# Layer 0 of a four-layer convolution network: the last 1x1 convolution on two pixel rows at once, with whole image rows for residual and result

## The chip, the cores and the metric

The kernel runs on one core of a Trainium2 chip. The metric is the device time of one execution in microseconds (us). A core has five engines, each with its own instruction queue that runs in order: TensorE (PE, with its weight loads PEld) multiplies matrices and writes PSUM, VectorE (DVE) and ScalarE (ACT) work element by element, GpSimd (POOL) and SyncE (SP) here mainly issue transfers (DMAs) between HBM and SBUF, the on-chip memory. An engine that waits holds up everything behind it in its own queue.

## The reference

Four layers, each `x = x + conv(groupnorm(x))`, on `x` of shape (4, 64, 256, 256) in f32. Only layer 0 is touched. Cut to what matters:

```python
x = einsum('bchw,oc->bohw', x, w_in)            # 64 -> 384 channels
xp = x in patches of 8 x 8
x = irfft2(rfft2(xp) * fft_filter), patches put back
x = conv(x, w_dw, 3x3, depthwise)
x1, x2 = split(x, 2, axis=1)
x = gelu(x1) * x2                               # 192 channels
return einsum('bchw,oc->bohw', x, w_out)        # 192 -> 64 channels
```

The layer's output is added to its input. Layer 1 then needs the mean and variance of that sum, so the kernel collects statistics of it while it is still on the chip.

## The kernel before

An image of 256 x 256 is 32 rows of 32 patches. Layer 0 works on 12 blocks (three for each image, `blocks`, index `p`), each of 11 rows of patches that begin one patch row apart from the image's edge (`i0` is -1, 10 or 21), so first and last blocks are cut at the edge: some pixel rows of them have 10 patch rows and not 11. Filter and depthwise convolution are one linear map from a patch (and its neighbours) to a patch, done as matrix products with the 64 pixels of a patch on the partitions.

For each block, four times (`kb`, 48 channel pairs each):

- `expand` (lines 444 to 463), for up to 12 patch rows `t`: PE multiplies the normalised input by `w_in` into two PSUM tiles; ACT copies one and DVE the other into `u` (L459 for even `t`, L461 to L463 for odd). Four PSUM tags (`p0` to `p3`, two banks each) go round, so the next `t` but one waits for these copies.
- `convolve` (L494, L503), for 12 groups `g`: 32 matmuls into two PSUM tiles, ACT takes the gelu (L510), DVE multiplies (L511), POOL stores the gated result to `g` in HBM (L514), one row of 374 = 11 x 34 columns for each of 64 pixels and 192 channels. `load_w` (L471) brings the weights three groups ahead.

The last convolution of block p-1 is worked into block p as 16 units (`unit`, `project`), one after `convolve` at g = 1, 4, 7 and 10. A unit is one pixel row `r` of the 8 in a patch and one half of its 8 pixels. `load_half` brings what a unit needs: the residual `r` (L559, one pixel row, the left half of the image's columns on partitions 0 to 63, the right half on 64 to 127) and `g` (L546, L550). A unit runs 16 matmuls (L591 with all 128 partitions, L598 with 64); each reads two pixels of up to 11 patch rows in runs of 8 columns, and writes every second word of PSUM, so that the result lies in the order of the image. DVE adds it to the residual (L607, or L610 and L612), three instructions of statistics follow after every second unit (L618), and POOL stores the row (L622). Each residual row or result is moved in pieces of 128 columns, 512 bytes.

After the last block a tail runs the 16 units of block 11 with nothing beside them (loop `p == NB`), with up to three pixel rows loaded ahead, on SP's and ACT's queues. Layer 1 begins behind it.

The order on PE, DVE, ACT and SP is the order of the program (`manual_schedule`), so where a call stands decides what stands ahead of it in each queue.

Of the kernel before, what the change touches and what calls it, by code (L numbers as in the profile page):

```python
# [17 lines left out]
C = 64  # L18
HID = 192
# [74 lines left out]
def _layouts(i):  # L94
# [6 lines left out]
    by_class = np.concatenate([turn[:, 0:2].ravel(), turn[:, 2].ravel()])  # L101
# [20 lines left out]
class _Net:  # L122
# [152 lines left out]
    def _layer0(self, ctx, dst):  # L275
# [36 lines left out]
        wts = [dr.tile([2, 64, 2, Q, NC], F32, name=f"wt{t}") for t in range(HID // C)]  # L312
# [63 lines left out]
        def weights(t, copies):  # L376

            for hh in range(2):
# [13 lines left out]
                for h in range(2):  # L392
                    for k, cols in ((0, [(0, 0, C), (C, 96, NC - C)]), (1, [(0, Q, NC)])):
                        for n0, c0, n in cols:
                            nc.gpsimd.dma_start(
                                wts[t][h, 32 * hh : 32 * hh + 32, k, :, n0 : n0 + n].rearrange("i c n -> c i n"),
                                T[quarters[2 * h + k], :, :, c0 : c0 + n].rearrange("p a b n -> p (a b) n"),
                            )
# [4 lines left out]
        xns, x0, wl, st, gs, bst0s, bst1, loads, rts = ({} for _ in range(9))  # L403
        xr = lambda v: v.rearrange("c (i r) w -> r c i w", r=P)
# [60 lines left out]
        def load_w(j):  # L465

            p, k = divmod(j, HID // 8)
            if p >= NB:
                return
            w = wl[j] = p_w.tile([128, 2, 4, NC], F32, tag="w", name=f"w_{j}")  # L470
            nc.sync.dma_start(  # L471
                w, wts[k // 8][:, :, :, 4 * (k % 8) : 4 * (k % 8) + 4].rearrange("h i k c n -> (h i) k c n")
            )
# [11 lines left out]
        def convolve(p, kb, g):  # L485
# [5 lines left out]
            for k in range(2):  # L491
                for c in range(2):
                    for h in range(2):
                        nc.tensor.matmul(  # L494
                            out(C * c, C, k, h), w[halves[h], k, 2 * (G % 2) + c, 0:C], cells(h, 4 * g + 2 * k + c, 0, 0),
                            start=True, stop=False, tile_position=(h * C, c * C), skip_group_check=True,
                        )
            for n, (c0, m, down, right) in enumerate(UNITS):
                for k in range(2):
                    for c in range(2):  # L500
                        q = C * c + Q * (1 - k)
                        for h in range(2):
                            nc.tensor.matmul(  # L503
                                out(q, m, k, h), w[halves[h], k, 2 * (G % 2) + c, c0 : c0 + m],
# [14 lines left out]
        def planes(r):  # L519

            if r < 5:
                return [(0, 6 * r, 0, 6), (1, 4 + 2 * r, 6, 2)]
            if r == 5:
                return [(0, 30, 0, 2), (1, 28, 2, 4), (1, 14, 6, 2)]
            return [(1, 16 + 6 * (r - 6), 0, 6), (1, 2 * (r - 6), 6, 2)]

        def rows_in(p, r):
# [3 lines left out]
            return lo, hi, i0 + lo + (r == P - 1), (r + 1) % P  # L531

        def load_g(p, r, half):

            pools, queues = sources[p == NB - 1], (nc.sync, (nc.sync, nc.scalar)[p == NB - 1])
            g1 = pools[0].tile([128, 4, L], F32, tag="g1", name=f"g1_{p}_{r}_{half}")
            g6 = pools[1].tile([128, 2, L], F32, tag="g6", name=f"g6_{p}_{r}_{half}")
            loads[p, r, half] = g1, g6
            q0 = 4 * half
            for x, p0, q, n in planes(r):  # L540
                part = lambda lo, m: (max(q, lo), min(q + n, lo + m))
                for k in range(2):
                    at = (x ^ k) * Q + p0 - q
                    lo, hi = part(q0, 4)
                    if lo < hi:
                        queues[k].dma_start(g1[halves[k], lo - q0 : hi - q0], gs[p][k, 0:C, at + lo : at + hi])  # L546
                    for s in range(2):
                        lo, hi = part(q0 + 2 * s, 2)
                        if lo < hi:
                            queues[k].dma_start(  # L550
                                g6[quarters[2 * s + k], lo - q0 - 2 * s : hi - q0 - 2 * s],
                                gs[p][k, C : HID // 2, at + lo : at + hi],
                            )

        def load_r(p, r):
            lo, hi, j0, rr = rows_in(p, r)
            rt = rts[p, r] = sources[p == NB - 1][2].tile([128, NR, HW2], F32, tag="r", name=f"r_{p}_{r}")[:, 0 : hi - lo]
            for s in range(2):
                nc.sync.dma_start(  # L559
                    rt[halves[s]], xr(a["x"][blocks[p][0]])[rr][:, j0 : j0 + hi - lo, s * HW2 : (s + 1) * HW2]  # L560
                )

        def load_half(p, r, half):
            if 0 <= p < NB and r < P:
                if half == 0:
                    load_r(p, r)
                load_g(p, r, half)

        def project(p, r, half):

            b, i0 = blocks[p]
            lo, hi, j0, rr = rows_in(p, r)
            m = hi - lo
            po, rt = banks(f"po_{p}_{r}_{half}"), rts[p, r]
            n = m * 16

            def moving(g, bank, s, x):
                at = lambda q: (O1 + 8 * s, E1 + 1 + 8 * s)[x] if q < 7 else (E1 + 8 * s, O1 + 8 * s)[x]
                o, d = at(2 * bank), at(2 * bank + 1) - at(2 * bank)
                return bass.AP(  # L580
                    tensor=g.tensor, offset=g.offset + lo * CW + o, ap=[g.ap[0], [L + d, 2], [CW, m], [1, 8]]
                )

            out = lambda bank, s, x: po[halves[s], bank, 0 : 2 * n].rearrange(
                "p (q i j x) -> p x q i j", q=2, i=m, x=2
            )[:, x]
            g1, g6 = loads.pop((p, r, half))
            for k in range(2):
                for x in range(2):
                    for s in range(2):  # L590
                        nc.tensor.matmul(  # L591
                            out(k, s, x), wo1, moving(g1[:, 2 * k], 2 * half + k, s, x),
                            start=(x == 0), stop=False, skip_group_check=True,
                        )
            for x in range(2):
                for k in range(2):
                    for s in range(2):
                        nc.tensor.matmul(  # L598
                            out(k, s, x), wo6[halves[k]],
                            moving(g6[halves[k], 0], 2 * half + k, s, x),  # L600
                            start=False, stop=True, tile_position=(k * C, s * C), skip_group_check=True,
                        )
            rv = rt.rearrange("p i (j w) -> p w (i j)", w=P)
            pv = po[:, 0:2, 0 : 2 * n].rearrange("p b (k n) -> p b k n", k=2)
            if half == 0:
                v = rv[:, 1:5].rearrange("p (b k) n -> p b k n", k=2)
                nc.vector.tensor_add(v, v, pv)  # L607
                return
            v = rv[:, 5:7]
            nc.vector.tensor_add(v, v, pv[:, 0])  # L610
            v = bass.AP(tensor=rv.tensor, offset=rv.offset + 7, ap=[rv.ap[0], [-7, 2], rv.ap[2]])
            nc.vector.tensor_add(v, v, pv[:, 1])  # L612
# [3 lines left out]
            for k in range(0, m, 4):  # L616
                v = rt[:, k : min(k + 4, m)].rearrange("p i w -> p (i w)")
# [868 lines left out]
```

## Time and profile before

| | us |
|---|---|
| median of 3 runs | 6655.79 |
| lowest, highest | 6634.38, 6662.45 |
| the profiled execution | 6626.21 |
| its span, first to last instruction | 6624.4 |
| layer 0: first `convolve` starts, last one ends | 146.6, 3937.0 |
| the tail: until the last matmul of L598 ends | 4061.3 |
| first matmul of layer 1 | 4077.8 |

A page of the profile lists busy times by engine, the span in 40 slices, the DMA queues, the chain of work that ended last, and groups of instructions. A matmul in f32 appears as two records. Matmuls on different parts of the array run side by side, so what a group of them costs is read from start to start in the timeline, not from the length of a record. "Idle before" names what an engine waited for. "issue" is idle time for which the profile shows no cause.

| engine in layer 0, 500 to 3500 us | busy us of 3000 |
|---|---|
| PE | 2783 |
| DVE | 1725 |
| ACT | 1251 |
| DMA engines, mean share | 0.78 |

### The profile page before, as it was taken

Reading aid. Unit: us, or ns where it says so; the run is one execution under the profiler, and the core shown is the slowest. Engines: PE = TensorE matmul, PEld = TensorE weight load, DVE = VectorE, ACT = ScalarE, POOL = GpSimd, SP = SyncE. Lnnn points to the kernel's source line nnn. Section 1 sums busy time; section 2 is a strip of 40 time slices with the busy share of each in tenths; the row PEclk is TensorE's granted clock in tenths of the full one; section 3 lists DMA queues with packets and bytes.
Section 4 is the critical chain, followed back from the end, with each engine's and each line's share of the span. In section 5 each row is a group of like instructions: output and inputs, shape, how many; then the busy total and the mean of one; then the engine's idle time right before and its main releaser. Section 6 shows DMA issues by size and latency. Waiting matters only on the chain.

```text
span 6624.4 us, 238282 instructions
## 1 busy us (share of the span) xinstructions
PE 6040.5 (91%) x106712; PEld 3213.7 (49%) x106712; DVE 4275.7 (65%) x5924; ACT 3238.8 (49%) x4564; POOL 1050.4 (16%) x1646
## 2 busy tenths in 40 slices
PE   2999999999999999999999986999899999999987
PEld 1455555555555555555555543333344444443576
DVE  5556555555555555555555545999798898885355
ACT  4454434344434444344444422777777887783211
POOL 3111111111111111111111111111022222221011
PEclk9999999999999999999999997999999999999855
DMA  8577777777878877877767669999666666677889
GB/s 236 152 206 211 216 213 222 218 216 213 230 213 238 219 222 207 223 214 220 210 193 206 188 194 247 232 229 228 165 177 176 168 180 173 173 187 264 318 351 394
DMA packets 878510, 1447.67 MB, mean 219 GB/s; under 512 B 77252, under 2 KB 586452, under 8 KB 875444
## 3 DMA queue, kind: packets, MB, share of 16 engines
q1 hardware_dynamic: 725284, 923.09, 54.8%
q0 software_dynamic: 148672, 500.14, 21.7%
q8 instruction: 843, 13.81, 0.9%
q10 hardware_dynamic: 3536, 9.20, 0.5%
q14 instruction: 175, 1.43, 0.1%
HBM read 932.08 MB, written 500.04 MB: 216 GB/s over the span
## 4 chain that ended last, share of the span: by engine, by line
PE 82%; DMA 6%; ACT 5%; DVE 3%; issue 3%; SPq 0%; POOL 0%; ACTq 0%; DVEq 0%; POOLq 0%
PE pc L503 18%; PE pc L494 12%; PE m L869 10%; PE psu L444 9%; PE one L1110 8%; PE div L1069 6%; PE po L591 4%; ACT u L459 4%; PE psu L450 4%; PE psz L1099 2%; PE po L598 2%; DMA x<-x 2%; PE psa L1297 2%; DMA g<-g 2%; PE psy L1444 1%
## 5 line engine op out<-in xcount | busy, mean ns | idle before, releaser
L511 DVE TENSOR_TENSOR h<-h,pc 128x374 f32<-128x374 f32 x1152 | 574.7, 541 | 1268.7 <-ACT h L510 1267.7
L510 ACT ACTIVATE h<-pc 128x374 f32<-128x374 f32 x1152 | 492.6, 480 | 1824.9 <-PE pc L503 1822.0
L503 PE MATMUL pc<-u,w 64*16 64x374 f32 (+2 forms) x27648 | 1244.1, 483 | 0.0
L494 PE MATMUL pc<-u,w 64*64 64x374 f32 x9216 | 928.6, 494 | 81.1 <-DVE u L463 32.2
L514 POOL DMA_DIRECT2D g<-h x576 | 416.7, 723 | 3111.0 <-DVE h L511 2904.7
L503 PEld LDWEIGHTS pc<-u,w 64*16 64x16 f32 (+2 forms) x27648 | 413.8, 92 | 769.5 <-issue 768.9
L444 PE MATMUL psu<-win,xn 64*128 64x96 f32 x8704 | 627.0, 283 | 131.8 <-ACT u L459 110.5
L459 DVE COPY u<-psu 64x384 f32<-64x384 f32 x1088 | 604.3, 555 | 167.7 <-PE psu L444 155.7
L459 ACT COPY u<-psu 64x384 f32<-64x384 f32 x1088 | 560.0, 515 | 238.9 <-PE psu L444 218.8
L444 PEld LDWEIGHTS psu<-win,xn 64*128 64x128 f32 x8704 | 574.0, 192 | 202.6 <-ACT u L459 143.6
L1055 DVE TENSOR_TENSOR q<-xn 128x2313 f32<-128x2313 f32 (+2 forms) x256 | 627.4, 2492 | 1.7 <-ACT xn L256 1.7
L1110 PE MATMUL one<-z,wp 32*32 32x512 f32 x16384 | 592.1, 596 | 17.8 <-issue 13.6
L494 PEld LDWEIGHTS pc<-u,w 64*64 64x64 f32 x9216 | 350.3, 133 | 531.0 <-issue 354.7
L256 ACT ACTIVATE xn<-x,nb,r 128x1024 f32<-128x1024 f32 (+3 forms) x272 | 486.8, 1793 | 244.6 <-DMA x<-x 140.8
L1056 ACT ACTIVATE q<-q 128x2313 f32<-128x2313 f32 (+2 forms) x256 | 529.0, 2086 | 32.7 <-DVE q L1055 31.2
L450 PE MATMUL psu<-win,xn 64*64 64x96 f32 x17408 | 458.2, 252 | 81.9 <-issue 57.2
L1069 PE MATMUL div<-q,ones 64*32 64x512 f32 x8192 | 466.3, 594 | 12.9 <-ACT q L1056 9.3
L1110 PEld LDWEIGHTS one<-z,wp 32*32 32x32 f32 x16384 | 367.6, 103 | 223.6 <-issue 80.1
L450 PEld LDWEIGHTS psu<-win,xn 64*64 64x64 f32 x17408 | 395.5, 137 | 126.0 <-issue 77.0
L1143 POOL DMA_DIRECT2D x<-r x512 | 275.5, 547 | 969.8 <-DVE r L1140 945.1
L591 PE MATMUL po<-g,wo 128*64 128x176 f32 (+1 forms) x3072 | 315.8, 348 | 63.3 <-DMA g<-g 41.3
L869 PE MATMUL m<-t,wk 64*64 64x512 f32 x3072 | 341.1, 588 | 0.0
(162 smaller groups left out, 6668.1 us busy)
## 6 DMA issues: line engine op xcount, KB each, us to landing
g<-h POOLq DMA_DIRECT2D x576, 374.0 KB, 7.0
x<-x SPq DMA_DIRECT2D x240, 640.0 KB, 6.4
w<-wt SPq DMA_DIRECT2D x288, 448.0 KB, 8.4
x<-x SPq DMA_DIRECT2D x100, 1024.0 KB, 14.2
g<-g SPq DMA_DIRECT2D x414, 187.0 KB, 5.7
g<-g SPq DMA_DIRECT2D x736, 93.5 KB, 6.0
x<-in_x_dram SPq DMA_DIRECT2D x256, 256.0 KB, 8.1
x<-o POOLq DMA_DIRECT2D x128, 512.0 KB, 8.2
```

Source lines behind the costliest of these rows:

```text
L444: nc.tensor.matmul(ps[s][:, k, at], xn[halves[s], n : n + 2].rearrange("p n r w -> p (n r w)"), win[halves[s], kb, 0 : 2 * PB], start=True ...
L450: nc.tensor.matmul(ps[s][halves[1 - odd], k, at], xn[halves[s], n + odd].rearrange("p r w -> p (r w)"), win[halves[s], kb, PB * (1 - odd) ...
L459: copy(at(h, 8 * s + o), v[k, c : c + PB])
L494: nc.tensor.matmul(out(C * c, C, k, h), w[halves[h], k, 2 * (G % 2) + c, 0:C], cells(h, 4 * g + 2 * k + c, 0, 0), start=True, stop=False, ...
L503: nc.tensor.matmul(out(q, m, k, h), w[halves[h], k, 2 * (G % 2) + c, c0 : c0 + m], cells(h, 4 * g + 2 * k + c, down, right), start=False, ...
L511: nc.vector.tensor_mul(h[:, k], h[:, k], ps[k][:, 1, 0:L])
L591: nc.tensor.matmul(out(k, s, x), wo1, moving(g1[:, 2 * k], 2 * half + k, s, x), start=(x == 0), stop=False, skip_group_check=True,)
L869: nc.tensor.matmul(rows2(m)[halves[j], s], w[dx][halves[s]], ts[n][halves[s], i, 2 * j : 2 * j + 2, dx : dx + W], start=(dx == 0), stop=(d ...
L1055: nc.vector.tensor_sub(d, p0, p1)
L1056: nc.scalar.activation(d, d, AF.Square)
L1069: ins = nc.tensor.matmul(ps[quarters[j], h], ones[halves[h]], q[n, g, k][halves[h], r + 2 * j : r + 2 * j + 2, o : o + W], start=(m == 0), ...
L1110: ins = nc.tensor.matmul(rows2(ps[g])[quarters[j], k], w[quarters[i]], z[quarters[i], h, 2 * j + dy : 2 * j + dy + 2, dx : dx + W], tile_p ...
```

## The change

- A unit is now two pixel rows (`r` = 2k and 2k+1) and two of the 8 pixels. Row 2k goes to the lower 64 partitions of PSUM, row 2k+1 to the upper. `project` runs 8 matmuls, each over a whole gated row of 374 columns, and writes 374 columns in one piece; pad columns are computed too and left in PSUM. DVE picks the wanted columns out when it adds: two instructions for each unit, four where the two rows have different patch rows (the last pair of rows in first and last blocks).
- Residual and result tiles hold whole image rows (1024 bytes), one tile for four units, with one buffer in place of two of half the size (in the tail two in place of three). `load_r` stands in `expand` at t = 8, not at a unit.
- `load_g` brings four transfers for most units; one takes 96 partitions and one 32. The order of rows in `w_out` (`by_class`) follows.
- The statistics of a tile (six, or twelve where the rows differ) are put in a list (`tasks`) and taken from it: two after each `convolve` that has no unit behind it, one after each `t` of `expand`. Units now follow g = 0, 3, 6 and 9; the tile is complete at g = 9, so the list is taken at g = 10 (two), g = 11 (two), t = 0 and t = 1 (one each).
- The weights lie in HBM so that a load reads 3584 bytes in one piece and not two of 1792.

```diff
-        wts = [dr.tile([2, 64, 2, Q, NC], F32, name=f"wt{t}") for t in range(HID // C)]
+        wts = [dr.tile([2, 64, Q, 2, NC], F32, name=f"wt{t}") for t in range(HID // C)]
...
+        def load_g(p, n):
+            if not (0 <= p < NB and n < 16):
+                return
+            rr, q0 = (2 * (n // 4), 2 * (n // 4) + 1), 2 * (n % 4)
+            last = p == NB - 1
+            pools, queues = sources[last], (nc.sync, (nc.sync, nc.scalar)[last])
+            g1 = pools[0].tile([128, 2, 2 * L], F32, tag="g1", name=f"g1_{p}_{n}")
+            g6 = pools[1].tile([128, 2, L], F32, tag="g6", name=f"g6_{p}_{n}")
+            loads[p, n] = g1, g6
+            parts = [(g1[Q:128], 1, slice(0, HID // 2), q0, 2), (g1[0:Q], 0, slice(C, HID // 2), q0, 2)]
+            parts += [(g6[halves[q]], 0, slice(0, C), q0 + q, 1) for q in range(2)]
...
+        def load_r(p, n):
+            if not (0 <= p < NB and n < P // 2):
+                return
+            rt = rts[p, n] = sources[p == NB - 1][2].tile([128, NR, W], F32, tag="r", name=f"r_{p}_{n}")
             for s in range(2):
+                lo, hi, j0, rr = rows_in(p, 2 * n + s)
+                nc.sync.dma_start(rt[halves[s], lo:hi], xr(a["x"][blocks[p][0]])[rr][:, j0 + lo : j0 + hi])
...
+            for q in range(2):
+                for s in range(2):
+                    nc.tensor.matmul(
+                        po[halves[s], q, 0:L], wo1, g1[:, s, q * L : (q + 1) * L],
+                        start=True, stop=False, skip_group_check=True,
+                    )
+            for q in range(2):
+                for s in range(2):
+                    nc.tensor.matmul(
+                        po[halves[s], q, 0:L], wo6[halves[q]], g6[halves[q], s],
+                        start=False, stop=True, tile_position=(q * C, s * C), skip_group_check=True,
+                    )
...
+                    v = bass.AP(
+                        tensor=v.tensor, offset=v.offset + lo * CW + even,
+                        ap=[v.ap[0], [CW, m], [odd - even, 2], [1, W // P // 2]],
+                    )
+                    o = rt[h, lo:hi].rearrange("p i (j x w) -> p w i x j", x=2, w=P)[:, (q0 + q + 1) % P]
+                    nc.vector.tensor_add(o, o, v)
+            if n % 4 < 3:
                 return
+            for side in sides:
+                h, lo, hi, j0, rr = side
+                nc.gpsimd.dma_start(xr(dst[b])[rr][:, j0 + lo : j0 + hi], rt[h, lo:hi])
...
+            tasks.extend((stats, next(slot), c) for c in chunks)
...
-            p_r = pool("l0r", 2, side="right")
+            p_r = pool("l0r", 1, side="right")
...
-                    sources.append([pool("l0g1e", 6), pool("l0g6e", 6), pool("l0re", 3)])
-                    ahead = 3
+                    sources.append([pool("l0g1e", 6), pool("l0g6e", 6), pool("l0re", 2)])
+                    ahead = 6
+                    for n in range(2):
+                        load_r(p - 1, n)
...
                         if 0 <= i0 + t < NP:
                             expand(p, kb, t)
+                        task()
+                        if t == 8:
+                            load_r(p - 1, kb)
...
-                        if g in (1, 4, 7, 10):
+                        if g in (0, 3, 6, 9):
                             unit()
+                        else:
+                            task(2)
```

## The prediction

> **What bounds the kernel now.** I read the slices and the chain first. PE is busy through layer 0 (slices 2 to 24), and the chain of what ended last is mostly PE.
>
> ```profile
> PE   2999999999999999999999986999899999999987
> ...
> PE pc L503 18%; PE pc L494 12%; PE m L869 10%; PE psu L444 9%; PE one L1110 8%; PE div L1069 6%; PE po L591 4%; ACT u L459 4%; PE psu L450 4%; PE psz L1099 2%; PE po L598 2%; DMA x<-x 2%; PE psa L1297 2%; DMA g<-g 2%; PE psy L1444 1%
> ```
>
> Then the table of stretches, to separate the loop (first row) from the tail (second). Columns after the window: its length, then busy us of PE, PEld, DVE, ACT, POOL; granted clock, DMA share, GB/s.
>
> ```profile
> 500.00:3500.00 3000.00, 2783.34 (x53660) 1579.50 (x53662) 1724.83 (x3021) 1250.62 (x2468) 449.56 (x606) 0.98 0.78 216
> 3949.00:4062.00 113.00, 61.24 (x512) 37.90 (x512) 34.45 (x44) 0.00 (x0) 11.32 (x17) 0.59 1.02 248
> ```
>
> In the loop PE is the bound, in the tail DMA (1.02). Where PE idles in the loop is in PE's waits from 430 to 3900 us: inside `expand`, and at the first matmul behind it, always on the copies or on "issue". No DMA is among its larger waits.
>
> ```profile
> PE psu L444 <- ACT u L459: 99.2, 152, 1.5
> PE psu L450 <- issue: 54.6, 46, 4.2
> PE pc L494 <- DVE u L459: 28.3, 15, 2.0
> PE pc L494 <- DVE u L463: 27.1, 27, 1.3
> ```
>
> So PE sets the pace in `convolve` and in units; in `expand` it is the ring PE, copies, PE. A second of work saved on PE in a unit counts in full. A second added to DVE counts in `expand` and hardly elsewhere.
>
> **The matmuls of a unit.** PE's timeline, start to start. A unit of 11 patch rows, one of 10, and in layer 1 matmuls with 512 columns in long runs:
>
> ```profile
> 1181.91 1.62 PE L591 MATMUL po<-g,wo 128*64 128x176 f32 x16
> 1183.46 0.93 PE L598 MATMUL po<-g,wo 64*64 64x176 f32 x16
> 1184.21 1.48 PE L494 MATMUL pc<-u,w 64*64 64x374 f32 x16
> ```
>
> ```profile
> 432.04 1.48 PE L591 MATMUL po<-g,wo 128*64 128x160 f32 x16
> 433.45 0.86 PE L598 MATMUL po<-g,wo 64*64 64x160 f32 x16
> 434.13 1.48 PE L494 MATMUL pc<-u,w 64*64 64x374 f32 x16
> ```
>
> ```profile
> 4255.18 1.04 PE L869 MATMUL m<-t,wg 64*64 64x512 f32 x8
> 4256.04 1.04 PE L869 MATMUL m<-t,wi 64*64 64x512 f32 x8
> ```
>
> A unit costs 1184.21 - 1181.91 = 2.30 us, or 434.13 - 432.04 = 2.09. L591's 16 records go two side by side (8 rounds of 1.55/8 = 0.194 us for 176 columns; one by one they would take 0.55 ns a column, less than any row here), L598's four side by side (4 rounds). The new unit has 8 and 8 records: 4 + 2 = 6 rounds of 374 columns. In layer 1, 8 records are 2 rounds of 0.43 us, 0.84 ns a column, so 374 cost 0.314 and the unit 6 x 0.314 = 1.89. The other end: a `convolve` takes 3.52 us (1187.69 to 1191.22) for 10 rounds of 374 columns in runs of 17, 0.352 a round, unit 2.11. I take 1.89, since the new rows are read and written in one run, as in layer 1. The loop holds the units of blocks 0 to 10: 176, of which 62 read 10 rows (31 pixel rows of the four first and three last blocks) and 114 read 11. Saving 114 x 0.41 + 62 x 0.20 = **59 us**; at 2.11 it is 114 x 0.19 - 62 x 0.02 = 20.
>
> **The statistics on DVE.** Before, L618 stands between the product of g = 10 and that of g = 11, where DVE waits for ACT anyway. Now part of it is queued behind the product of g = 11, ahead of the first copies of `expand`. DVE's timeline there, before:
>
> ```profile
> 635.10 1.61 DVE L618 BATCH_NORM_STATS2 bst<-r 128x6 f32<-128x512 f32 x3
> 637.51 1.00 DVE L511 TENSOR_TENSOR h<-h,pc 128x374 f32<-128x374 f32 x2 [0.81 <-ACT h L510]
> 638.98 2.26 DVE L459 COPY u<-psu 64x384 f32<-64x384 f32 x4 [0.47 <-PE psu L444]
> ...
> 643.42 2.26 DVE L459 COPY u<-psu 64x384 f32<-64x384 f32 x4 [0.45 <-PE psu L444]
> ```
>
> A pair of patch rows takes 4.44 us (638.98 to 643.42, and the next at 647.86). The ring is: copies of even t (2.26), PE's next even t (1.96), 0.2 of delay; DVE is idle for 0.45 of each pair. PE starts the next even t only when the copies are done, and the first matmul of `convolve` waits for the last copy, so what delays DVE beyond its idle time is not won back. Two statistics cost 1.28 (L320: 2 in 1.28), one of 256 elements 1.61 - 1.28 = 0.33. With 11 rows: 1.28 - 0.47 = 0.81 ahead of the first copy, then 0.64 + 0.33 - 0.45 = 0.52 behind t = 0 and 1: 1.33. With 10 rows 0.81 + 0.66 - 0.45 = 1.02. Where the last tile has twelve: 2.56 - 0.47 + 0.97 + 0.66 - 0.45 = 3.27. Of the 44 tiles of the loop 43 have an `expand` behind them: 12 x 1.02 + 24 x 1.33 + 7 x 3.27 = 67 us. PE's "issue" stalls (54.6 and 18.7 us, 1.7 for each of these `expand`) let DVE catch up when they fall into the first third: 43/3 x 0.5 = 7. I take **+60**. The ends: 0 if it all goes into other idle time of DVE (1275 of 3000 us in the loop, though most lies in `convolve`); 12 x 1.94 + 24 x 2.25 + 7 x 4.19 = 107 if nothing of it is absorbed.
>
> The adds: 8 x 0.81 (L610, 352 elements) for four units against 2 x (1.46 + 0.81 + 0.81), 6.5 against 6.2, and up to 3 us at once where there are four. They lie beside `convolve` plus unit (3.52 + 1.89 = 5.41) with the product (1.0) and L320 (1.28): 3.9 in 5.4, hidden. Without that cover they would cost what they last, 0.3 x 44 = 13 more than before.
>
> **Loads in the loop.** At zero. SP: `load_r` waits at the head of SP's queue for the tile's stores and statistics, since there is one buffer. The stores go to POOL behind the adds of g = 9, some 4 us after that `convolve`, and land 7.5 us after issue (L622's median; twice the size now, say 10): 8 us into `expand`. The statistics end at about the same time. The load lands 10 us later, at 18 of 28 us, and the first add comes 3.5 + 1.9 us after `expand`: some 15 us in hand. Behind it in SP's queue stand L471 and L546's successors; weights are three groups (21 us) ahead. At a new block the first `load_g` waits for the last store of `g` (before: SP held from 713 to 727 us) and the residual comes behind it; two units and one tile are 3.7 MB, at 248 GB/s 15 us, so 742; the first `convolve` there started at 745.2, the first add comes at 751: 9 us in hand. If the cover is gone, DVE waits, then the products behind it, then ACT's and PE's tiles. The weights' runs, POOL's fewer stores and fewer SP instructions shorten what PE does not wait for.
>
> **The tail.** DMA shares from 3948 to 4062 us (first two rows; packets, MB, share of 16 engines), and of layer 1 from 4200 to 4600 us (third):
>
> ```profile
> q1 hardware_dynamic: 13584, 14.14, 57.1%
> q10 hardware_dynamic: 3456, 8.81, 29.9%
> ```
>
> ```profile
> q1 hardware_dynamic: 50087, 50.03, 65.5%
> ```
>
> q10 carries `g` alone: 0.299 x 16 x 114 us / 3456 = 158 ns for packets of 2549 bytes. Priced by bytes like that, the 9.2 MB of `g` on q1 take 567 of its 1041 us; the 9728 residual packets of 512 bytes have the rest, 49 ns each. In layer 1 a packet of 1000 bytes takes 84 ns. So a 1024-byte row costs 84 to 98 and not 98: 5632 rows x 14 ns / 16 engines = 5 us less. `g` is cut finer (2992 and 1496 bytes; by the line through 49 and 158 ns, 182 and 102): 1.5 us of engine time for each of 16 units, over 16 engines 1.5 more. Two tiles of residual (2.8 MB) are asked for while the last `g` store lands (3937 to 3949 us) in place of 1.45 MB: 1.35 MB / 248 GB/s = 5.5 less. The last twelve statistics (7 us) and adds (3) lie in the 12 us that layer 1 waited for `x` after the last unit. Sum **-9**, between 0 and -20.
>
> [...]
>
> **Sum.** 6626.2 - 59 + 60 - 9 = 6618 for the profiled execution. It stands 29.6 under the median of the runs shown, so 6648 there: **no change that can be told** (0.5%, 33 us, is about what a measurement of this kernel can tell).
>
> **Rivals.** (a) The statistics hide: DVE has 4 to 5 idle us in each `expand`, and PE's stalls give more. For: idle on paper. Against: it comes in pieces of 0.45 that the ring needs. Then 6655.8 - 59 - 9 = 6588. (b) Slower: nothing of them is absorbed, the ring at the start of `expand` takes 107: 6655.8 - 59 + 107 - 9 = 6695. It decides from (33 + 59 + 9) / 43 = 2.35 us for a tile, where I have 1.4. For: every copy that ends `expand` is DVE's (L463, L459). (c) Fewer bytes in flight end PE's "issue" stalls: in block 0, with DMA shares of 0.09 to 0.36 in `expand`, there are none; later, at 0.55 to 0.89, 1.7 us each. Half of 73 gone: 6648 - 37 = 6611. Against: the DMA time of a block falls by some 9 us of 310 (residual 5, weights 24 x 128 packets fewer at 22 ns / 16 = 4). (d) The rows gain less than layer 1's long runs say (unit 2.11, saving 20): 6648 + 39 = 6687.
>
> **Chances and range.** Forecast 0.48; (a) and (c) and their mixes 0.27; (b), (d) and their mix 0.25. Range 6595 to 6700: from near (a) to just above (b). The likeliest one alone: 6625 to 6675.
>
> **What would show it.** Unit start to start 1.89 us (L591's and L598's successors); L618 ahead of L459 at the start of `expand`, and `expand` 1 to 3 us longer from first matmul to the second part of the first L494; tail some 9 us shorter. Wrong if adds wait for the residual, if `expand` is no longer, or if "issue" shrinks.

## The result and the profile after

The changed kernel takes 6811.47 us (median, 6805.40 to 6818.67) against 6658.82 before (6634.38 to 6662.45): 1.024 times, 95% interval 1.0222 to 1.0258, some 153 us slower. The forecast was 6648. The profiled execution spans 6816.8 us against 6624.4, 192.4 more. That is some 40 more than the medians differ: the profiled execution of the kernel before (6626.21) lies under all four of the runs above.

After: the busy slices of PE, and the chain of what ended last, by line (L495 and L504 are the matmuls of `convolve`, L445 and L451 those of `expand`, L582 and L588 those of a unit).

```profile
PE   3999999889999999999999894999999999999987
...
PE pc L504 17%; PE pc L495 12%; PE m L885 10%; PE one L1126 8%; PE psu L445 7%; PE div L1085 6%; PE psu L451 4%; PE po L582 4%; DVE u L460 3%; DMA x<-x 2%; PE psz L1115 2%; PE po L588 2%; DVE bst L618 2%; PE psa L1313 2%; ACT u L460 2%
```

Two entries are new among those shown: copies (L460) and statistics (L618) of DVE. The table of stretches, the loop and then the tail (length; busy us of PE, PEld, DVE, ACT, POOL; granted clock, DMA share, GB/s):

```profile
500.00:3500.00 3000.00, 2717.93 (x48830) 1462.43 (x48832) 1693.36 (x3039) 1193.32 (x2353) 375.41 (x508) 0.95 0.77 207
4113.00:4226.00 113.00, 51.51 (x264) 15.48 (x256) 28.92 (x46) 0.85 (x2) 5.88 (x10) 0.68 1.05 258
```

In the loop PE is busy for 65 us less of 3000 (2783 before), and the granted clock fell from 0.98 to 0.95: PE waits more, and while it works it works more slowly. Where it waits, from 430 to 4100 us (us in total, times, longest):

```profile
PE psu L451 <- issue: 112.8, 50, 4.9
PE psu L445 <- ACT u L460: 64.7, 100, 0.8
PE psu L445 <- DVE u L460: 39.1, 57, 2.2
PE pc L495 <- DVE u L460: 32.1, 16, 2.0
PE psu L445 <- issue: 31.7, 15, 4.0
```

"issue" was 54.6 and 18.7 us before, and the wait of L445 for DVE's copies is as good as new (0.5 us before). Both are in `expand`. From the timelines of both kernels, stretch by stretch: the 44 `expand` of the blocks with units last 1547 us in place of 1346 (+201; first matmul to the second part of the first `convolve`); the stretches between them 2120 in place of 2146 (-26); from the last `convolve` to the first matmul of layer 1 it is 149.4 in place of 140.7 (+9); the start of the loop and layer 1 differ by 2 and 8. So all of the loss is in `expand`, whose code the change hardly touches. Some 30 of the 201 us may come from which executions were profiled: in e7 below, whose `expand` is that of before, it lasts 1378 us in an execution of 6666.74 us.

**One of these `expand`, at 1748 us.** PE's timeline (start, us, instruction; idle before and its releaser), then SP's queue, then a table of stretches with granted clock and DMA share in the third and second column from the end.

```profile
1752.52 0.46 PE L445 MATMUL psu<-win,xn 64*128 64x96 f32 x2 [0.79 <-ACT u L460]
1755.19 2.29 PE L445 MATMUL psu<-win,xn 64*128 64x96 f32 x30 [2.22 <-DVE u L460]
1757.41 3.18 PE L451 MATMUL psu<-win,xn 64*64 64x96 f32 x64
...
1764.36 1.06 PE L451 MATMUL psu<-win,xn 64*64 64x96 f32 x41 [0.47 <-issue]
1765.35 2.33 PE L445 MATMUL psu<-win,xn 64*128 64x96 f32 x32
1767.61 1.37 PE L451 MATMUL psu<-win,xn 64*64 64x96 f32 x53
1773.85 0.90 PE L451 MATMUL psu<-win,xn 64*64 64x96 f32 x11 [4.87 <-issue]
1774.68 3.73 PE L445 MATMUL psu<-win,xn 64*128 64x96 f32 x32
1778.34 2.63 PE L451 MATMUL psu<-win,xn 64*64 64x96 f32 x64
1780.90 2.03 PE L445 MATMUL psu<-win,xn 64*128 64x96 f32 x32
```

```profile
1756.47 4.58 SPq L553 DMA_DIRECT2D g<-g  x8
1761.59 1.73 SPq L565 DMA_DIRECT2D r<-in_x_dram  x2
1764.30 1.46 SPq L472 DMA_DIRECT2D w<-wt  x1
```

```profile
1757.00:1760.00 3.00, 2.93 (x56) 2.50 (x58) 2.88 (x7) 2.07 (x4) 0.00 (x0) 0.50 0.85 205
...
1769.00:1772.00 3.00, 0.00 (x0) 0.00 (x0) 0.97 (x2) 0.71 (x2) 0.00 (x0) 1.00 1.15 202
1772.00:1775.00 3.00, 1.15 (x14) 0.93 (x14) 0.21 (x1) 0.45 (x1) 0.00 (x0) 0.80 1.16 199
1775.00:1778.00 3.00, 3.00 (x32) 3.00 (x30) 1.46 (x3) 1.09 (x3) 0.00 (x0) 0.50 0.54 133
```

Three things are seen. The late copies leave PE idle for 2.22 us at 1753, and the next 64 matmuls take 3.18 us where 1.55 is normal: the clock is 0.50. `g`, residual (1.4 MB) and weights are then asked for within 10 us, the 16 DMA engines are full (1.15), and PE stands for 4.87 us although no semaphore or engine that the trace shows holds it ("issue"). And again the clock is at 0.50 behind it: 32 matmuls in 3.73 us in place of 2.03. Both gaps cost more than their own length: 1.63 us over the 1.55 and 1.70 over the 2.03. In the 44 `expand` the granted clock stood at 0.50 for 352 us, before for 106 (in e7 for 175).

**What "issue" stands for here.** Before, PE's timeline around 1050 us, and the page's line for the queue that carries instructions (packets, MB, share):

```profile
1046.39 0.48 PE L450 MATMUL psu<-win,xn 64*64 64x96 f32 x9
1048.53 1.38 PE L450 MATMUL psu<-win,xn 64*64 64x96 f32 x55 [1.66 <-issue]
1049.84 2.03 PE L444 MATMUL psu<-win,xn 64*128 64x96 f32 x32
1051.80 1.05 PE L450 MATMUL psu<-win,xn 64*64 64x96 f32 x39
1053.87 0.79 PE L450 MATMUL psu<-win,xn 64*64 64x96 f32 x25 [1.02 <-issue]
```

```profile
q8 instruction: 843, 13.81, 0.9%
```

Between the two stalls lie 55 + 32 + 39 = 126 matmuls, as after the change between 1764.36 and the stall of 4.87 us (41 + 32 + 53). The kernel's 106712 matmuls over 843 packets are 127 a packet, and after the change 103640 over 818 are 127 too. So PE stalls where one packet (13.81 MB / 843, 16 KB) of its instructions ends and the next has not come. In `expand` 126 matmuls last 4.3 us (1048.53 to 1052.85), in `convolve`, 64 in 3.52 us, about 6.9.

The profile's records of DMA packets show when such a packet starts. Windows 1045.9 to 1046.0 and 1051.3 to 1051.4 before, then 1764.4 to 1770.75 and 1770.75 to 1770.85 after (packets that start there, MB, share of 16 engines; the third window has no row of q8):

```profile
q8 instruction: 1, 0.02, 63.1%
q8 instruction: 1, 0.02, 66.6%
q1 hardware_dynamic: 1065, 1.35, 110.3%
q8 instruction: 1, 0.02, 86.6%
```

The share, times 16 engines, times the 0.1 us of the window, is how long the packet took: 1.01, 1.07 and 1.39 us. They ended near 1047.0, 1052.4 and 1772.2, and PE went on 1.4 to 1.7 us behind each (1048.53, 1053.87, 1773.85). All 376 stalls of 1.8 us or more put down to "issue" in the 44 `expand` of the 20 traces ended like that, 1.2 to 2.0 us behind the end of such a packet; of all matmuls of `expand` about one in nine stands there. The packet itself is not slow; it starts late. In the third window, 6.4 us from PE's first matmul of one packet, the next has not started, and the engines are full (1.10). Behind all stalls of 0.5 us or more, the next packet starts 1.3 us (median) after PE began the one before it where the DMA engines are under 0.6 busy meanwhile (392 cases), and 4.2 us where they are over 1.1 (155). With the packet's 1.0 to 1.3 us and some 1.45 from its end to the first matmul that makes about 3.8 or 7 us, against the 4.3 us for which a packet lasts in `expand` and the 6.9 in `convolve`.

### The profile page after: what moved, and what is told of

Its sections match the earlier page's. It is cut to its first block, busy times and chain, and to the rows that moved or that the text cites. A ratio compares the mean times of both kernels' runs of the same rounds, so it can differ in the third digit from the quotient of the medians.

```text
span 6816.8 us, 230910 instructions
## 1 busy us (share of the span) xinstructions
PE 6125.5 (90%) x103640; PEld 3143.8 (46%) x103640; DVE 4340.0 (64%) x6132; ACT 3236.8 (47%) x4564; POOL 976.1 (14%) x1550
## 3 DMA queue, kind: packets, MB, share of 16 engines
q1 hardware_dynamic: 641396, 926.12, 54.6%
## 4 chain that ended last, share of the span: by engine, by line
PE 79%; DVE 9%; DMA 6%; issue 4%; ACT 2%; SPq 0%; DVEq 0%; POOLq 0%; ACTq 0%
PE pc L504 17%; PE pc L495 12%; PE m L885 10%; PE one L1126 8%; PE psu L445 7%; PE div L1085 6%; PE psu L451 4%; PE po L582 4%; DVE u L460 3%; DMA x<-x 2%; PE psz L1115 2%; PE po L588 2%; DVE bst L618 2%; PE psa L1313 2%; ACT u L460 2%
## 5 line engine op out<-in xcount | busy, mean ns | idle before, releaser
L504 PE MATMUL pc<-u,w 64*16 64x374 f32 (+2 forms) x27648 | 1239.3, 482 | 0.2 <-issue 0.2
L495 PE MATMUL pc<-u,w 64*64 64x374 f32 x9216 | 928.6, 494 | 80.0 <-DVE u L460 32.1
L445 PE MATMUL psu<-win,xn 64*128 64x96 f32 x8704 | 678.7, 298 | 154.8 <-ACT u L460 75.4
L504 PEld LDWEIGHTS pc<-u,w 64*16 64x16 f32 (+2 forms) x27648 | 412.5, 92 | 766.8 <-issue 766.8
L445 PEld LDWEIGHTS psu<-win,xn 64*128 64x128 f32 x8704 | 617.8, 207 | 230.6 <-ACT u L460 102.3
L460 DVE COPY u<-psu 64x384 f32<-64x384 f32 x1088 | 604.0, 555 | 185.1 <-PE psu L445 171.6
L460 ACT COPY u<-psu 64x384 f32<-64x384 f32 x1088 | 559.6, 514 | 340.5 <-PE psu L445 320.6
L451 PE MATMUL psu<-win,xn 64*64 64x96 f32 x17408 | 521.1, 270 | 153.1 <-issue 113.5
L495 PEld LDWEIGHTS pc<-u,w 64*64 64x64 f32 x9216 | 351.6, 133 | 577.4 <-issue 328.6
L451 PEld LDWEIGHTS psu<-win,xn 64*64 64x64 f32 x17408 | 450.4, 150 | 204.8 <-issue 154.4
L606 DVE TENSOR_TENSOR r<-r,po 128x352 f32<-128x352 f32 (+3 forms) x448 | 317.9, 743 | 213.4 <-PE po L588 144.6
L582 PE MATMUL po<-g,wo 128*64 128x374 f32 x1536 | 294.0, 503 | 57.0 <-DMA g<-g 47.0
## 6 DMA issues: line engine op xcount, KB each, us to landing
x<-in_x_dram SPq DMA_DIRECT2D x256, 256.0 KB, 10.1
```

Source lines behind the costliest of these rows:

```text
L445: nc.tensor.matmul(ps[s][:, k, at], xn[halves[s], n : n + 2].rearrange("p n r w -> p (n r w)"), win[halves[s], kb, 0 : 2 * PB], start=True ...
L451: nc.tensor.matmul(ps[s][halves[1 - odd], k, at], xn[halves[s], n + odd].rearrange("p r w -> p (r w)"), win[halves[s], kb, PB * (1 - odd) ...
L460: copy(at(h, 8 * s + o), v[k, c : c + PB])
L495: nc.tensor.matmul(out(C * c, C, k, h), w[halves[h], 2 * (G % 2) + c, k, 0:C], cells(h, 4 * g + 2 * k + c, 0, 0), start=True, stop=False, ...
L504: nc.tensor.matmul(out(q, m, k, h), w[halves[h], 2 * (G % 2) + c, k, c0 : c0 + m], cells(h, 4 * g + 2 * k + c, down, right), start=False, ...
L582: nc.tensor.matmul(po[halves[s], q, 0:L], wo1, g1[:, s, q * L : (q + 1) * L], start=True, stop=False, skip_group_check=True,)
```

## The experiments

Four theories were tried against each other: the late statistics (L618 ahead of the copies of `expand`); the place of the residual load, in `expand`; its form (whole rows, 704 KB at once, bytes in flight); other parts of the change.

**e1: statistics early, the rest as changed.** `task()` in `expand` is taken out, and

```diff
-                        else:
-                            task(2)
+                        if g == 9:
+                            task(3)
+                        if g == 10:
+                            task(len(tasks))
```

> The changed kernel with the statistics of a residual tile taken where before's were: three behind the product of g=9 and the rest behind that of g=10 (L618), none at g=11 and none between the copies of expand. First theory (the statistics hold up the copies of u, the matmuls of expand wait, and what follows them, the matmuls' lower granted clock and the 'issue' stalls, comes from that): most of the lost time comes back, 6640 to 6690 us against 6811. Second theory (the residual load of 1.4 MB, which the single buffer pushes into a few us of expand, starves the matmuls): little comes back, only the 20 to 50 us in which copies were seen waited for, 6760 to 6795 us, and the 'issue' stalls between 18 and 27 us after the start of an expand stay at over 100 us in all.

6786 us, 1.0224 (1.0198 to 1.0251), an interval that overlaps the changed kernel's. As the second theory has it, but the edit was weak: with the unit still at g=9, DVE now holds back the product of g=11, and PE waits 25 us for `h` at the start of `expand` in place of 39 for the copies. It doesn't clear the statistics.

**e2: no residual loads in the loop.** The first tile is loaded once and all later results are added into it, so the sums are not the reference's. In `load_r`:

```diff
+            if (p, n) > (0, 0) and p < NB - 1:
+                rts[p, n] = rts[0, 0]
+                return
...
```

> The changed kernel without the residual loads of the loop: the first tile is loaded once and all later results of blocks 0 to 10 are added into it and stored from it (only the last block, after the loop, loads its own residuals). Left out are 43 loads of 1.4 MB, so its result is not the reference's. Second theory (the load that falls into expand starves the matmuls): most of the lost time comes back, 6640 to 6700 us, and the 'issue' stalls of expand fall from 148 us to 80 or less. First theory (statistics on VectorE): 6780 to 6810 us, expand stays some 4 us longer than before's.

6663 us, 1.0043 (1.0029 to 1.0056): 131 us of the loss are gone. PE's waits show which:

```profile
PE psu L445 <- DVE u L460: 38.7, 57, 2.2
...
PE psu L451 <- issue: 29.6, 25, 3.3
```

"issue" at L451 falls from 112.8 to 29.6 us; the waits for late copies (38.7) stay, and `expand` is still 55 us longer than before (1401).

**e3: the kernel before with late statistics.** They are put in a list as in the change and taken from it behind g=11 (two) and behind the `t` of `expand` (one each):

```diff
+                        task()
...
+                        if g == 11:
+                            task(2)
+                        elif g < 10:
+                            task(3)
```

> The kernel before with one edit: the three statistics that it takes with the last unit of a kb (at g=10) are put off, two of them behind the product of g=11 and one behind the first copy of the next expand; units, loads and stores stay. First theory: a delay of VectorE at the start of expand is enough by itself to slow what follows, so the time rises by 80 us or more (6740 to 6850). Second theory: it costs only what the copies are late, 3 x 1.1 us in 44 expands less what is absorbed, 20 to 60 us (6680 to 6720).

6662 us, 1.0040 (1.0024 to 1.0056): 27 us, too little for the first theory alone.

**e4: e1 and e2 at once.**

> The changed kernel with both edits: statistics at g=9 and g=10, and the residual loads of the loop left out as in the run without them (its result is not the reference's). Both theories: nothing of the 192 us is left, and the shorter units (2.08 us in place of 2.30 and 2.09) and the shorter tail show, about 40 us under before: 6600 to 6640. If it stays above 6700, a third cause is at work (the units at g=0, the finer loads of g, the result's store as 1.4 MB at once, or the weight runs). If the two single edits give back parts that add up to this one's, the causes are separate; if each alone gives back nearly all, they are one chain.

6662 us, 1.0045 (1.0030 to 1.0061), the same as e2 and not 40 under before: something else costs, too. PE's waits for `h` (25 us) don't explain it, since e5 below has as many (29) and is 37 us faster. PE's "issue" in the waits is larger, 51.3 + 12.1 us against e5's 29.2 + 4.0; what makes it so isn't shown (the profiled execution is e4's slowest).

**e5: the load in the convolution, all statistics early.** The load waits for the first matmul of g=0, the units move:

```diff
+                        ins = convolve(p, kb, g)
+                        if g == 0:
+                            load_r(p - 1, kb, ins)
...
-                        if g in (0, 3, 6, 9):
+                        if g in (2, 4, 6, 8):
                             unit()
-                        else:
-                            task(2)
+                        if g > 8:
+                            task(3)
```

> The changed kernel with all its residual loads, but each waits for the first matmul of the convolution g=0 instead of being free to start in expand; the units stand behind g=2, 4, 6, 8 and all statistics behind g=9 and g=10. If the place of the 1.4 MB load (in expand) is the cause: 6600 to 6670 us, expand within 60 us of before's 1346 in all, 'issue' stalls of expand at 80 or less. If the load costs wherever it lies (its bytes, or one transfer of 704 KB in place of two of 352): 6740 or more.

6638 us, 0.9989 (0.9975 to 1.0003): with the same bytes and rows the whole loss is gone. `expand` is at 1351, "issue" at L451 is 29.2. The edit moves the load, the units and the statistics at once; e8 and e14 take them apart.

**e6: the kernel before with both residual rows asked for in `expand`**, `load_r(p - 1, r)` for rows 2kb and 2kb + 1 at t=8, none behind the units.

> The kernel before with one edit: the residual loads of both pixel rows of a kb (the same 1.4 MB in the same 352 KB pieces) are put at t=8 of the expand ahead, where the changed kernel has them, instead of behind the units. If the place of the load is the cause: it takes most of the change's loss over, 80 to 160 us on before's 6632 (6710 to 6790), with 'issue' stalls of expand at 120 or more. If the loss needs the changed kernel's larger rows or its later statistics: 6625 to 6660.

6634 us, 0.9985 (0.9971 to 1.0000). A miss: the place alone does not do it. But the load was not as bunched: the first of its four pieces started 4.0 us into `expand` (median of 44), the last at 8.3; the changed kernel's two start at 9.8 and 10.6.

**e7: the kernel before with the weights' layout of the change.**

> The kernel before with the weight layout of the change alone (runs of 3584 bytes). The prediction had it at zero: 6620 to 6645 us. If the 29 us that are left without residual loads come from the weights: 6650 to 6670.

6633 us, 0.9992 (0.9970 to 1.0014): nothing, as predicted.

**e8: e5 with units at g = 3, 5, 7, 9 and the statistics as changed**, `task(2)` at the other g and `task()` in `expand`.

> As the run with the load in the convolution, but units behind g=3, 5, 7, 9, and the statistics taken as the change does (two behind each of the convolutions without a unit, the last of them between the copies of the next expand). The prediction's price of late statistics was 60 us; the kernel before with late statistics lost 27. If they cost that here too: 20 to 60 us over the run with early statistics. If the statistics only cost where the load lies in expand as well: within 10 us of it.

6697 us, 1.0080 (1.0056 to 1.0103): 59 us over e5. This is the price of late statistics without the load, units one group later included, and PE's wait for DVE is back (2.5 us in e5):

```profile
PE psu L445 <- DVE u L460: 37.2, 58, 3.1
```

**e9: the kernel before, both rows gated on the first matmul of t=3** (`self.after(d, ins)`).

> The kernel before with both residual rows of a kb (1.4 MB in 352 KB pieces of half rows) asked for together, when the first matmul of expand's t=3 starts (about 8 us into expand, the moment at which the changed kernel's load starts; in the earlier run with the load in expand the first 0.7 MB started at 2 us and the rest when its buffer came free). If the bytes in flight at once are the cause (instructions of TensorE's queue wait behind them): 'issue' stalls of expand at 110 us or more, time 60 to 130 us over before. If the whole rows of 704 KB in one piece, or something else of the changed kernel, are needed: within 20 us of before.

6651 us, 1.0012 (0.9999 to 1.0026): the bytes at that moment cost this kernel hardly anything. The theory of bytes in flight, as stated, falls.

**e10: the changed kernel's load in two steps**, one half from t=3, the other from t=7.

> The changed kernel with its residual load still in expand and still from one buffer, but in two steps: one half (704 KB) from t=3, the other from t=7 (about 10 us later); nothing else moved. If the bytes in flight at once are the cause: the 'issue' stalls fall to 90 us or less and the time comes down by 80 to 130 us, to 6680 to 6730. If any residual load in expand costs, however it is cut: 6780 or more.

6725 us, 1.0121 (1.0101 to 1.0142): 79 us back, "issue" in `expand` at 76. So in the changed kernel it does matter how much is asked for at once.

**e12: the changed kernel's load in half rows**, four pieces of 352 KB:

```diff
-                nc.sync.dma_start(rt[halves[s], lo:hi], xr(a["x"][blocks[p][0]])[rr][:, j0 + lo : j0 + hi])
+                for c in (slice(0, HW2), slice(HW2, W)):
+                    nc.sync.dma_start(rt[halves[s], lo:hi, c], xr(a["x"][blocks[p][0]])[rr][:, j0 + lo : j0 + hi, c])
```

> The changed kernel with its residual loads cut into half rows, four of 352 KB as before had them, in place of two of 704 KB; place and bytes stay. If the whole rows are what starves the matmuls: 6680 to 6720. If it is the bytes in flight and their place: 6790 to 6850, no better than the changed kernel, since runs of 352 bytes take the queues no less time.

6761 us, 1.0180 (1.0157 to 1.0202): between the two; 40 us come from the form alone. (A half row is 128 f32, 512 bytes; the "352 bytes" above and in e16 below is a slip.)

**e13: e3 and e9 at once.**

> The kernel before with both edits at once: its three last statistics of a kb put off into g=11 and expand (alone: 30 us more), and the 1.4 MB of residual asked for at t=3 of expand (alone: 10 us more). If the two make each other worse (the late copies leave TensorE at a lower granted clock and behind, and the load then meets it there), as the changed kernel suggests: 80 us or more over before, 6720 and up. If they only add up: 30 to 50 us over before, 6670 to 6695; then the changed kernel's 158 us need its own rows or units.

6678 us, 1.0070 (1.0053 to 1.0087): 44 us for 27 and 8. They add up; they do not make each other worse.

**e14: the changed kernel's units and loads, load gated on t=3 of `expand`, but units at g = 0, 2, 4, 6 and statistics at 8, 9, 10.**

> The changed kernel's units, rows and whole 704 KB loads, with the load in expand at t=3 as in the changed kernel, but the units behind g=0, 2, 4, 6 and the statistics two each behind g=8, 9, 10, so that nothing of them is left on VectorE when expand begins. If it takes both, late statistics and the load in expand, to lose much: 6635 to 6670 us. If whole rows loaded in expand are enough by themselves: 6710 to 6780.

6716 us, 1.0139 (1.0109 to 1.0168). Without late statistics, whole rows in `expand` cost 0.0150 more than the same rows in the convolution (e5), 100 us; the units stand at other groups in the two. PE's waits, and the landing times of its residual pieces between 1000 and 3500 us (count, KB, median us):

```profile
PE psu L446 <- ACT u L461: 95.9, 144, 1.6
PE psu L452 <- issue: 94.7, 39, 5.4
```

```profile
r<-in_x_dram SPq DMA_DIRECT2D x39, 704.0 KB, 9.9
```

Hardly a wait for late copies is left (0.7 us); "issue" is.

**e15 to e18** take e14 with the weights in runs of 1792 bytes, with the residual in half rows, with both, and e9 with weight runs of 3584 bytes.

> The run with early units and the load in expand (82 us over before), with the weights in runs of 1792 bytes as before had them. If long runs are what keeps TensorE's instructions waiting (each piece of an instruction fetch takes its turn behind longer packets): 6650 to 6690 us, 'issue' stalls of expand at 90 or less. If not: 6700 to 6730.

> The same run (82 us over before) with the residual loads as half rows of 352 bytes, four of 352 KB. In the changed kernel itself this gave 40 us back. If the length of the residual's rows is the cause: 6650 to 6690. If not: 6700 to 6740.

> The same run with both: weights in runs of 1792 bytes and residual in half rows, so that the bytes asked for in expand are cut as in the kernel before with the load at t=3 (10 us over before). If the length of the packets in flight is the cause: 6630 to 6665. If it stays at 6690 or more, the units (their loads of g, or their place) are what is needed beside the load.

> The kernel before with the residual asked for at t=3 of expand (10 us over before) and the weights in runs of 3584 bytes (alone: no change). If long packets in flight behind the residual are the cause: 30 to 70 us over before. If not: within 20 us of before.

6731 us, 1.0146 (1.0117 to 1.0175); 6673, 1.0059 (1.0040 to 1.0077); 6688, 1.0079 (1.0054 to 1.0105); 6648, 1.0023 (1.0002 to 1.0044). The weights' runs do nothing in either kernel. Half rows give 0.0080 back, 53 us. e16's pieces:

```profile
r<-in_x_dram SPq DMA_DIRECT2D x78, 352.0 KB, 8.5
```

Side by side (landing as above; idle of PE put down to "issue", of 1.8 us or more, in the 44 `expand`, counted in the timelines):

| run | load | landing us | such gaps, their sum us | `expand` us | ratio |
|---|---|---|---|---|---|
| before | behind units | 8.0 | 11, 26 | 1346 | 1 |
| e9 | half rows, t=3, before's units | 7.4 | 17, 43 | 1374 | 1.0012 |
| e5 | whole rows, g=0 | 7.2 | 5, 13 | 1351 | 0.9989 |
| e16 | half rows, t=3 | 8.5 | 27, 80 | 1420 | 1.0059 |
| e14 | whole rows, t=3 | 9.9 | 37, 113 | 1456 | 1.0139 |
| after | whole rows, late statistics | 10.1 | 38, 124 | 1547 | 1.0240 |

In the four runs with the load inside `expand` (7.4 to 10.1 us), the longer it takes to land, the more often and the longer PE lacks instructions (17 to 38 gaps, 43 to 124 us). The columns scatter, though: e7, with the load behind the units, has 17 such gaps, 46 us and 1378 in the execution that was profiled, so e9's row can't be told from before's.

**e11: a version to beat both.** e5 with units at g = 2, 4, 5, 7, statistics at 8, 9, 10, and in the tail

```diff
-pool("l0g1e", 6), pool("l0g6e", 6), pool("l0re", 2)
+pool("l0g1e", 5), pool("l0g6e", 5), pool("l0re", 3)
...
-                        if n % 4 == 1 and n > 4:
-                            load_r(p - 1, n // 4 + 1)
+                        if n in (1, 5):
+                            load_r(p - 1, 2 + n // 4)
```

> The run with the load in the convolution, with two more edits: units behind g=2, 4, 5, 7 and the statistics two each behind g=8, 9 and 10; and in the tail three residual buffers, so that the last two residual tiles are asked for behind units 1 and 5 in place of 5 and 9. In the changed kernel's tail VectorE gets its last residual 5 us behind the last unit and ends 31 us behind it. If that lag is the tail's bound: 8 to 20 us less there, and 5 to 15 us from the waits for the product h at the start of expand (29 us): 6605 to 6630, 0.3 to 0.6% under before. If DMA bounds the tail whatever the order: 6630 to 6645.

6628 us, 0.9982 (0.9971 to 0.9992): 12 us under before and, by the ratios, 171 under the changed kernel. Less than this kernel's measurement can tell in one comparison of a few runs, but the interval excludes no change. From the last `convolve` to layer 1 it takes 132.9 us (140.7 before, 149.4 after).

## Why the prediction was wrong, step by step

**"Loads in the loop. At zero."** This step failed. Its argument was that the adds would not wait for the residual, and they don't: no wait of the loop names it. What was not asked is who else needs the DMA engines during those 10 us: TensorE's own instructions. e2 puts the loads in the loop at 131 us, e14 against e5 their place (with the units' groups) at 100. The prediction had a clue in rival (c), which tied "issue" to bytes in flight, but it expected fewer stalls, and its list of signs has "issue" shrinking, not growing; the one buffer put 1.4 MB into the middle of `expand`, where PE eats a packet of instructions in 4.3 us, and the stalls doubled (76 to 149 us), the long ones with half clock behind them.

**Statistics, +60.** The size held: e8 against e5, 59 us. In part that is luck: in the kernel before such a delay cost 27 (e3), and the working was incomplete. In the change L445 waits 57 times for DVE's copies; 50 of these waits are of 0.7 us or less, and the other seven, at the tiles with twelve statistics, are of 2.2 us, each with the clock at 0.50 behind it, which the working has not. DVE's timeline at the start of an `expand` after the change shows the queue as predicted:

```profile
1072.92 1.00 DVE L512 TENSOR_TENSOR h<-h,pc 128x374 f32<-128x374 f32 x2 [1.33 <-ACT h L511]
1073.84 1.87 DVE L618 BATCH_NORM_STATS2 bst<-r 128x6 f32<-128x512 f32 x3
1075.62 0.54 DVE L462 COPY u<-psu 128x384 f32<-128x384 f32 x1
```

**Unit, 1.89 us, saving 59.** Mis-sized; it is 2.08 to 2.09 (1193.24 - 1191.15):

```profile
1191.15 1.48 PE L582 MATMUL po<-g,wo 128*64 128x374 f32 x8
1192.56 0.86 PE L588 MATMUL po<-g,wo 64*64 64x374 f32 x8
1193.24 1.48 PE L495 MATMUL pc<-u,w 64*64 64x374 f32 x16
```

A round of 374 columns in one run takes 0.348 us, as rounds in runs of 17 do (0.352): the long runs brought nothing here, and the time was not in proportion to columns (0.93 ns each at 374, 0.84 at 512). The other end of the bound, 2.11, was right. The stretches between `expand` became 26 us shorter, near the 20 that this end gave.

**Tail, -9.** It is +9. PE's part did become shorter (last `convolve` to last unit 111.9 us in place of 124.2), but behind the last unit the wait grew from 16.5 to 37.4. DVE's timeline there (the last unit ends at 4225):

```profile
4230.04 0.74 DVE L606 TENSOR_TENSOR r<-r,po 64x352 f32<-64x352 f32 x1 [13.38 <-DMA r<-in_x_dram]
4233.63 2.15 DVE L606 TENSOR_TENSOR r<-r,po 64x320 f32<-64x320 f32 x3 [2.85 <-DMA r<-in_x_dram]
4235.79 1.02 DVE L618 BATCH_NORM_STATS2 bst<-r 128x6 f32<-128x512 f32 x2
4236.82 8.81 DVE L606 TENSOR_TENSOR r<-r,po 64x352 f32<-64x352 f32 x12
4245.66 7.61 DVE L618 BATCH_NORM_STATS2 bst<-r 64x6 f32<-64x512 f32 x12
```

The last tile's residual waits for a free one of two buffers and lands after all units, so sixteen adds and fourteen statistics stand in a row at the end, where the prediction laid them beside a wait for `x`. In e11 the residual is there in time, and four adds and the statistics are left:

```profile
4046.06 2.93 DVE L610 TENSOR_TENSOR r<-r,po 64x352 f32<-64x352 f32 x4 [0.61 <-PE po L592]
4049.03 7.61 DVE L622 BATCH_NORM_STATS2 bst<-r 64x6 f32<-64x512 f32 x12
```

**Weights and adds, zero.** e7, e15 and e18 agree on the weights; no wait of PE in the loop names an add.

The sum with measured terms: 6648 + 33 (unit, 59 - 26) + 131 (loads) + 18 (tail) = 6830, against 6811.

**Left open.** Why the same half rows at the same time cost the changed kernel (e16) 5 parts in a thousand more than the kernel before (e9). Where the DMA engines were over 1.1 busy, the next packet of instructions started 4.8 us (median of 11) after PE began the one before it in e16, and 3.2 (of 8) in e9. The units' loads of `g`, fewer and larger and at other moments, differ between them; that was not tried. Nor is it known what e4 pays for over e5.

## What to carry over

Ask of a transfer that moves not only whether its consumer will wait, but what else the DMA engines serve at that moment. Here TensorE's instructions came over them too (818 packets of 16 KB after the change), and a packet lasted 4.3 us in the short matmuls of `expand` against about 6.9 in `convolve`; the same load cost 100 us less beside the long matmuls (e5) than in `expand` (e14), the units' groups included. In these traces the rows behind a gap of TensorE of 1.8 to 2.4 us took 1.6 us longer on average than at full clock. Work on VectorE that was put behind the last product of a stage was paid at the start of the next: 27 us in e3, 59 in e8.

## What the runs showed of the hardware

Behind PE's gaps the granted clock was often at 0.50. In the `expand` of all 20 traces, the profile's records have it there within 2 us behind 106 of the 3860 gaps under 1.2 us, 138 of 182 between 1.8 and 2.4 us, and all 176 of 3 us or more (in the traces of before and after alone 28 of 519, 32 of 53, and all 22). The next three rows of the timeline then took longer than at full clock, by 1.6 us on average behind gaps of 1.8 to 2.4 us and by 2.5 us behind those of 3 us or more. From 430 to 3930 us the stretches at 0.50, 27 before and 61 after, last 3.41 us or two to four times that. Over the 3.41 us ahead of each, PE was busy for 5 to 66% before (median 53) and for 0 to 66% after (median 41): it had not always stood still. The gap of 2.22 us above is such a case; the 3.41 us ahead, with PE busy for 1.54, and the 3.41 at 0.50 (length; busy us of PE, PEld, DVE, ACT, POOL; granted clock, DMA share, GB/s):

```profile
1753.33:1756.74 3.41, 1.54 (x28) 1.58 (x29) 3.31 (x7) 0.71 (x2) 0.00 (x0) 1.00 0.37 140
1756.74:1760.15 3.41, 3.34 (x64) 2.91 (x64) 3.28 (x8) 2.07 (x4) 0.00 (x0) 0.50 0.79 193
```
